# A two-layer sandwich kernel: the residual moved to VectorE, the flag count and the next block's norms moved in the order, the last store on another queue

## The chip, the cores and the metric

The kernel runs on one core of a Trainium2 chip. The metric is device time in microseconds for one execution; each run of a program gives one time, and a kernel's time is the median of its runs. A core has five engines that run side by side and meet through semaphores: TensorE (PE in the profile; its weight loads are PEld), VectorE (DVE), ScalarE (ACT), GpSimd (POOL) and SyncE (SP), which here only issues transfers. Each engine takes its instructions in the order in which the program lists them. PSUM is the small memory that TensorE writes its products to, in banks; SBUF is the working memory; DRAM is the chip's main memory.

## The reference

The input is x with 4 x 512 rows of 512 numbers, so 2048 rows. Two feed-forward layers follow each other, each between two layer norms, with a residual around it:

```
x = x + norm(attn(norm(x)))        # first layer
x = x + norm(ffn(norm(x)))         # second layer

attn(h): s = silu(h @ Wg.T)        # 1376 wide
         set the 688 entries of each row with the smallest |s| to 0
         return (s * (h @ Wu.T)) @ Wd.T
ffn(h):  return (silu(h @ Wg.T) * (h @ Wu.T)) @ Wd.T
```

norm subtracts a row's mean and divides by the root of its variance plus 1e-5. All numbers are 32-bit floats.

## The kernel before

**Tiles.** A tile is 128 rows of x; there are 16, numbered 0 to 15. Weights stay in SBUF in 128-row pieces. Most products are done by a scheme with seven half-size products in place of eight (class `Seven`, L133, for the gate and up products; `downs`, L234, for the down product). Such a scheme needs sums of the quarters of both operands. Those of the weights are worked out once and kept in DRAM (`presum`), those of the activations come from VectorE (`moving_sums`, L125, tiles named T; L634 to L636 in `Unit.down_sums`) or from GpSimd (`stationary_sums`, L117, tiles named D). The products are called p1 to p7.

**First layer.** It runs in eight units of two tiles (class `Unit`). A unit norms and transposes its tiles, does the gate product, the up product and a search for each row's threshold (`search`, L467), and later the down product (`finish`, L644), the output norm and the residual. The search is a short fixed number of steps. For rows where it doesn't settle, it writes a flag into the tile `flags`. Whether any flag is set is counted once: L885 sums the flags of each partition, L887 sums over the partitions with a 1-column matmul into a bank named pbad, and L889 writes the count as an integer into `badi`. At L916 every engine reads this integer into a register, and at L917 all branch: with a count of 0, as here, past a second, general version of the whole program. The result of the first layer goes to DRAM as x1.

**Second layer.** It runs in four blocks of four tiles (class `Block`, L657). `norm(k)` (L663) loads tile k of x1 (into xnb, three buffers, L368), takes its statistics (L104, L106: st_ib, mv_ib), adds the epsilon (L108), takes the power -0.5 on GpSimd (L110), scales (L115), transposes on TensorE into a bank ptb (L376, of two banks with the tag pt) and copies with ScalarE into xT (L378; two buffers, one for each half of the columns). `sums` (L673) builds T. Then come five calls of `pair` (L685), each of which does the gate and the up product for 256 of the 1376 columns and ends with the multiplication L705; after each, `down_sums` (L724, L119 to L122) builds D on GpSimd. `rest` (L707) does the last 96 columns in the banks pxrb and pyrb with adds into sgr (L154, L160, L161, L167, L168). In the source the norms of the next block stand between `rest` and `finish` (L740), which does the down product for two pairs of tiles: padb, pydb and pxdb are the three banks of a pair, written by L260 and L266, and yb the two output tiles. The banks of the tags pa, px and py exist twice each, so pxdb of the second pair takes the bank that pxrb has used.

**Output norm.** `out_norm` (L344) loads the residual tile (xr or xrb, two buffers), takes mean and power of the row, and has three endings. In the first layer (`dst is x1`) VectorE subtracts the mean (L359) and does multiply-by-rs and add-residual in one instruction (L360). In the second layer, VectorE does subtraction and multiplication (L115, within `layernorm`) and GpSimd adds the residual (L363). The very last tile (`pa` given) has its first half still in PSUM: VectorE subtracts the mean from the two halves (L353) and does multiply and add in one instruction (L356). All three store with SP's queue (L364). All other loads and stores go by SP's queue too. The order of tiles at the end of the last block is 14, 12, 15, 13.

**Order.** The program is recorded in source order and then put in order by a scheduler, which simulates a timeline with its own costs and moves instructions of an engine ahead where it thinks they are ready (`tc.block(schedule_with_timeline_sim=True)`). So the norms of a block are not bound to the place where the source has them. In the built order of the kernel before, the first two tiles of a block are transposed at the start of the block before it, where they then keep the two pt banks, and VectorE takes their statistics there; those of tiles 4, 5 and 6 stand as early as the end of the first layer. The count of flags stands where the first layer ends, with a wait of SP's queue for it at 441 us.

Of the kernel before, what the change touches and what calls it, by code (L numbers as in the profile page):

```python
# [9 lines left out]
F32 = mybir.dt.float32  # L10
BF16 = mybir.dt.bfloat16
I32 = mybir.dt.int32
AF = mybir.ActivationFunctionType
ALU = mybir.AluOpType
AX = mybir.AxisListType

P = 128
# [14 lines left out]
def sandwich_kernel(  # L32
# [17 lines left out]
    nc = tc.nc  # L50
# [5 lines left out]
    NTT = NT // P  # L56
    TB = 4
# [12 lines left out]
    const = ctx.enter_context(tc.tile_pool(name="const", bufs=1))  # L70
    small = ctx.enter_context(tc.tile_pool(name="small", bufs=5))
# [7 lines left out]
    onec = const.tile([P, 1], F32, name="onec")  # L79
# [10 lines left out]
    flags = const.tile([P, 2, NTT], F32, name="flags")  # L90
    x1 = dram.tile([NT, H], F32, name="x1")
# [3 lines left out]
    def bank(tag, nm):  # L95
        return psum.tile([P, 512], F32, tag=tag, name=nm)

    def moments(parts, nm, kind):

        n = len(parts)  # L100
        bufs = 1 if kind == "f" else 5
        st = small.tile([P, n, 6], F32, tag="st" + kind, name=f"st_{nm}", bufs=bufs)
        for i in reversed(range(n)):
            nc.vector.bn_stats(st[:, i, :], parts[i])  # L104
        mv = small.tile([P, 2], F32, tag="mv" + kind, name=f"mv_{nm}", bufs=bufs)
        nc.vector.bn_aggr(mv, st)  # L106
        ve = small.tile([P, 1], F32, tag="ve" + kind, name=f"ve_{nm}", bufs=bufs)
        nc.vector.tensor_scalar(ve, mv[:, 1:2], EPS, None, ALU.add)  # L108
        rs = small.tile([P, 1], F32, tag="rs" + kind, name=f"rs_{nm}", bufs=bufs)
        nc.gpsimd.tensor_tensor(rs, ve, nhalf, ALU.pow)  # L110
        return mv, rs

    def layernorm(dst, src, nm, kind):
        mv, rs = moments([src], nm, kind)
        nc.vector.tensor_scalar(dst, src, mv[:, 0:1], rs, ALU.subtract, ALU.mult)  # L115
# [9 lines left out]
    def moving_sums(eng, b11, b12, b21, b22, t1, t2, t3, t4):  # L125

        eng.tensor_sub(t1, b12, b11)
        eng.tensor_sub(t2, b22, t1)
        eng.tensor_sub(t3, b22, b12)
        eng.tensor_sub(t4, b21, t2)  # L130
        return dict(p1=b11, p2=b21, p3=b22, p4=t4, p5=t1, p6=t2, p7=t3)
# [102 lines left out]
    def downs(work, pairs, key, w_d, wr, res, dst, nm, final=False):  # L234
# [81 lines left out]
        def p4(part=slice(None)):  # L316
            product("p4", PX, None, part)
            for p in st[part]:
                tiles, left, last, pa, px, py, ya, yb = p
                rest(px, p, 1, lo)  # L320
                nc.vector.tensor_add(yb[:, lo], yb[:, lo], px)
                out_norm(work, tiles[1], yb, res, dst, nm)
# [21 lines left out]
    def out_norm(work, t, y, res, dst, nm, pa=None):  # L344


        xr = work.tile([P, H], F32, tag="xr", name=f"xr{nm}_{t}")
        nc.sync.dma_start(xr, res[ts(t, P), :])
        if pa is not None:
            parts = [pa, y[:, H2:]]  # L350
            mv, rs = moments(parts, f"o{nm}_{t}", "f")
            for i in range(2):
                nc.vector.tensor_scalar(  # L353
                    y[:, ts(i, H2)], parts[i], mv[:, 0:1], None, ALU.subtract
                )
            nc.vector.scalar_tensor_tensor(y, y, rs, xr, ALU.mult, ALU.add)  # L356
        elif dst is x1:
            mv, rs = moments([y], f"o{nm}_{t}", "o")
            nc.vector.tensor_scalar(y, y, mv[:, 0:1], None, ALU.subtract)  # L359
            nc.vector.scalar_tensor_tensor(y, y, rs, xr, ALU.mult, ALU.add)  # L360
        else:
            layernorm(y, y, f"o{nm}_{t}", "o")
            nc.gpsimd.tensor_add(y, y, xr)  # L363
        nc.sync.dma_start(dst[ts(t, P), :], y)  # L364

    def load_x(work, src, t, nm, tag="xn", bufs=3):
        xn = work.tile([P, H], F32, tag=tag, name=f"xn{nm}_{t}", bufs=bufs)
# [12 lines left out]
    class Unit:  # L380
# [258 lines left out]
        def pair(self):  # L639
            return (  # L640
                self.tiles, lambda k, c: self.dleft[k][:, c, :], lambda i: self.hT[i][1]
            )

    def finish(units, wr):  # L644

        u = units[0]
        steps = downs(u.work, [u.pair() for u in units], "a", a_wd, wr, x, x1, u.nm)

        def p2():
            steps[-3]()  # L650
            for u in units:
                a12, s2 = u.dleft["p3"], u.dleft["p6"]
                nc.vector.tensor_sub(a12, a12, s2)

        return steps[:-3] + [p2] + steps[-2:]

    class Block:  # L657
# [27 lines left out]
        def pair(self, a, lefts):  # L685

            nm = f"{self.nm}_{self.b}_{a}"
            pool, kw = (self.work, dict(tag="hT")) if a < 2 else (self.big, dict(tag="b5"))
            hT = pool.tile([P, 2, N], F32, name=f"hTb{nm}", **kw)
            self.h.append(hT)  # L690
            h = hT.rearrange("p f (q n) -> p (f q) n", q=2)
            sg = self.work.tile([P, 4, N2], F32, tag="w", name=f"sg{nm}", bufs=1)
            ms = []
            for k, left, c in zip("gu", lefts, (sg, h)):
                left = {p: w[:, :, ts(a, P)] for p, w in left.items()}
                m = Seven(f"{k}b{nm}", left, self.right, c[:, 1, :], c[:, 2, :], c[:, 3, :])
                m.first()
                ms.append(m)
            c11g, c11u = [m.second() for m in ms]
            nc.scalar.activation(sg[:, 0, :], c11g, AF.Silu)  # L700
            nc.vector.tensor_mul(h[:, 0, :], sg[:, 0, :], c11u)
            ms[0].third()
            nc.scalar.activation(sg[:, 1:, :], sg[:, 1:, :], AF.Silu)  # L703
            ms[1].third()
            nc.vector.tensor_mul(h[:, 1:, :], sg[:, 1:, :], h[:, 1:, :])  # L705

        def rest(self, left):  # L707

# [31 lines left out]
        def finish(self, which, wr, final=False):  # L740
# [11 lines left out]
            for f in downs(self.work, pairs, "f", f_wd, wr, x1, out, f"b{self.nm}", final):  # L752
                f()

    def layers(nm, general):
        with ExitStack() as sctx:
            wpool = sctx.enter_context(tc.tile_pool(name="w" + nm, bufs=1))
# [9 lines left out]
            def last_rows(w_d, layer):  # L767
                n = I - 2 * HF
                w = work.tile([P, H], F32, tag="wr", name=f"wr{layer}{nm}", bufs=1)
                nc.sync.dma_start(w[:n, :], w_d[2 * HF :, :])  # L770
                return w[:n, :]

            blocks = [Block(b, nm, big, work) for b in range(NTT // TB)]
# [18 lines left out]
            for q in range(2):  # L792
                b = [
                    wu[:, 2 * r : 2 * r + 2, k * Q : (k + 1) * Q] for r in range(2) for k in (q, 2 + q)
                ]
                t = [y[:, :, ts(q, Q)] for y in (t1, t2, t4)]
                right.append(moving_sums(nc.vector, *b, t[0], t[1], b[1], t[2]))
            badi = None
            if general:
                wr = last_rows(a_wd, 1)  # L800
                ones = big.tile([P, I], BF16, tag="b5", name="g_ones")
# [12 lines left out]
            else:  # L814
                wr = last_rows(a_wd, 1)
# [64 lines left out]
            if not general:  # L880
                for f in units[-1].turns():
                    f()

                bad = small.tile([P, 1], F32, tag="bad", name="bad", bufs=2)
                nc.vector.tensor_reduce(bad, flags, AX.XY, ALU.add)  # L885
                pb = bank("pt", "pbad")
                nc.tensor.matmul(pb[:1, :1], bad, onec, start=True, stop=True)  # L887
                badi = const.tile([1, 1], I32, name="badi")
                nc.vector.tensor_copy(badi, pb[:1, :1])  # L889
                units[-1].down_sums()  # L890
                for f in finish([units[-1]], wr):
                    f()
            wr = last_rows(f_wd, 2)
            t = work.tile([P, 3, 2, I - 2 * HF], F32, tag="S", name=f"wrs{nm}", bufs=1)
# [5 lines left out]
            for b, block in enumerate(blocks):  # L900
                last = b + 1 == len(blocks)
                for a in range(HC):
                    block.pair(a, lefts)
                    block.down_sums(a)
                block.rest(rest)
                if not last:
                    for k in range(TB):
                        blocks[b + 1].norm(k)
                    blocks[b + 1].sums()
                block.finish([0, 1], wr, last)  # L910

        return badi

    with tc.block(schedule_with_timeline_sim=True):
        badi = layers("", False)
        nbad = nc.values_load(badi[0:1, 0:1], min_val=0, max_val=2 * P * NTT)  # L916
        with tc.If(nbad > 0, label="general"):  # L917
            layers("g", True)

# [35 lines left out]
```

## Time and profile before

| what | value |
|---|---|
| median of 3 runs | 875.24 us (874.98 to 875.84) |
| the profiled execution's own time | 873.69 us |
| its span, first to last instruction | 871.9 us |
| granted TensorE clock | 0.997 of full speed |
| TensorE busy | 855.0 us, 98% of the span |
| VectorE, ScalarE, GpSimd busy | 526.8, 302.8, 117.7 us |
| SP's transfers | 112.21 MB, 38.4% of the DMA engines' time |

The profile is of one execution. A line of the timeline gives the start (us from the span's start), the duration, the engine, the line of the source, the operation, and what it wrote and read (names without buffer numbers), with the partitions and elements of both, and how many of a kind follow each other. Brackets give the time that the engine had stood idle before, and what it waited for. SPq is a transfer's issue on SP; the transfer itself lands later. L12 means line 12 of the kernel, and line numbers are those of the kernel before unless the text says otherwise. VectorE, ScalarE and GpSimd being idle costs nothing in itself. The matmuls overlap: one of 256 columns is shown with 0.38 us, but the next starts 0.216 us after it.

### The profile page before, as it was taken

Reading aid. Unit: us, or ns where it says so; the run is one execution under the profiler, and the core shown is the slowest. Engines: PE = TensorE matmul, PEld = TensorE weight load, DVE = VectorE, ACT = ScalarE, POOL = GpSimd, SP = SyncE. Lnnn points to the kernel's source line nnn. Section 1 sums busy time; section 2 is a strip of 40 time slices with the busy share of each in tenths; the row PEclk is TensorE's granted clock in tenths of the full one; section 3 lists DMA queues with packets and bytes.
Section 4 is the critical chain, followed back from the end, with each engine's and each line's share of the span. In section 5 each row is a group of like instructions: output and inputs, shape, how many; then the busy total and the mean of one; then the engine's idle time right before and its main releaser. Section 6 shows DMA issues by size and latency. Waiting matters only on the chain. (4 is left out here: it accounts for less than half of the span.)

```text
span 871.9 us, 10340 instructions
## 1 busy us (share of the span) xinstructions
PE 855.0 (98%) x3642; PEld 659.8 (76%) x3642; DVE 526.8 (60%) x1417; ACT 302.8 (35%) x601; POOL 117.7 (14%) x193
## 2 busy tenths in 40 slices
PE   9999999999999999999999999999999999999995
PEld 5655566767667676678877888888888888888884
DVE  5887787776939587667956444454346442444424
ACT  3465575647474756565111111011111112011100
POOL 1000000000000000000112211321203221132102
PEclk9999999999999999999999999999999999999998
DMA  9998513335133333388473004510055001430032
GB/s 335 366 330 335 180 54 122 121 102 166 59 121 111 113 121 103 121 299 286 142 251 130 0 1 144 172 42 0 1 175 170 2 1 48 137 124 1 1 120 78
DMA packets 60381, 112.97 MB, mean 130 GB/s; under 512 B 4704, under 2 KB 34528, under 8 KB 60320
## 3 DMA queue, kind: packets, MB, share of 16 engines
q1 hardware_dynamic: 60320, 112.21, 38.4%
q8 instruction: 31, 0.51, 0.2%
q14 instruction: 30, 0.25, 0.1%
HBM read 93.32 MB, written 18.87 MB: 129 GB/s over the span
## 5 line engine op out<-in xcount | busy, mean ns | idle before, releaser
L488 ACT ACTIVATE ja<-v,cur 128x1376 bf16<-128x1376 f32 x96 | 138.4, 1441 | 56.6 <-DVE cur L513 36.9
L436 PE MATMUL pg<-wg,xT 128*128 128x456 f32 (+1 forms) x384 | 154.8, 549 | 0.2 <-ACT p L440 0.2
L436 PEld LDWEIGHTS pg<-wg,xT 128*128 128x128 f32 x384 | 71.9, 190 | 62.7 <-issue 57.6
L144 PE MATMUL pxub<-T,wu 128*128 128x256 f32 x160 | 41.3, 380 | 2.0 <-DVE hTb L160 1.8
L144 PE MATMUL pau<-wu,xT 128*128 128x344 f32 x128 | 43.1, 453 | 0.0
L144 PE MATMUL pagb<-xTb,wg 128*128 128x256 f32 x160 | 41.4, 379 | 0.0
L144 PE MATMUL paub<-xTb,wu 128*128 128x256 f32 x160 | 41.3, 380 | 0.0
L144 PE MATMUL pxgb<-T,wg 128*128 128x256 f32 x160 | 41.2, 380 | 0.0
L260 PE MATMUL pad<-wd_p,hT 128*128 128x256 f32 x160 | 38.9, 380 | 0.9 <-DMA wd_p<-in_L_attn_w_down_dram 0.9
L440 ACT ACTIVATE p<-pg 128x456 f32<-128x456 f32 (+1 forms) x48 | 26.0, 544 | 38.3 <-PE pg L436 35.0
L260 PE MATMUL pydb<-wdb_p,D 128*128 128x256 f32 x160 | 37.8, 379 | 0.0
L119 POOL TENSOR_TENSOR D<-hTb 128x256 f32<-128x256 f32 x20 | 14.6, 729 | 169.7 <-DVE hTb L705 169.7
L110 POOL TENSOR_TENSOR rs_o<-ve_o,nhalf 128x1 f32<-128x1 f32 x16 | 11.6, 724 | 188.6 <-DVE ve_o L108 188.5
L260 PE MATMUL pxd<-wd_p,hT 128*128 128x256 f32 x160 | 36.8, 379 | 0.0
L260 PE MATMUL padb<-wdb_p,hTb 128*128 128x256 f32 x160 | 36.7, 379 | 0.0
L260 PE MATMUL pxdb<-wdb_p,hTb 128*128 128x256 f32 x160 | 36.2, 379 | 0.0
L260 PEld LDWEIGHTS pad<-wd_p,hT 128*128 128x128 f32 x160 | 29.9, 190 | 7.5 <-DMA wd_p<-in_L_attn_w_down_dram 1.3
L144 PEld LDWEIGHTS pxub<-T,wu 128*128 128x128 f32 x160 | 30.1, 190 | 6.9 <-DVE hTb L160 2.2
L260 PEld LDWEIGHTS pxd<-wd_p,hT 128*128 128x128 f32 x160 | 30.4, 190 | 5.5 <-issue 0.4
L703 ACT ACTIVATE sg<-sg 128x768 f32<-128x768 f32 x20 | 16.9, 843 | 49.0 <-DVE sg L168 49.0
L493 DVE TENSOR_SCALAR low<-cur 128x2 int32<-128x2 f32 x48 | 7.9, 165 | 42.6 <-ACT ja L488 42.2
L260 PEld LDWEIGHTS padb<-wdb_p,hTb 128*128 128x128 f32 x160 | 30.4, 190 | 4.3
(246 smaller groups left out, 1715.6 us busy)
## 6 DMA issues: line engine op xcount, KB each, us to landing
wd_p<-sum_a SPq DMA_DIRECT2D x28, 640.0 KB, 4.0
wd_p<-in_L_attn_w_down_dram SPq DMA_DIRECT2D x21, 640.0 KB, 4.0
wdb_p<-sum_f SPq DMA_DIRECT2D x16, 640.0 KB, 4.0
wdb_p<-in_L_ffn_W_down_dram SPq DMA_DIRECT2D x12, 640.0 KB, 4.1
xn<-in_x_dram SPq DMA_DIRECT2D x16, 256.0 KB, 4.1
xr<-in_x_dram SPq DMA_DIRECT2D x16, 256.0 KB, 3.9
x<-y SPq DMA_DIRECT2D x16, 256.0 KB, 3.2
xnb<-x SPq DMA_DIRECT2D x16, 256.0 KB, 4.1
```

The costliest lines, as they stand in the source:

```text
L110: nc.gpsimd.tensor_tensor(rs, ve, nhalf, ALU.pow)
L119: eng.tensor_add(s1, a21, a22)
L144: nc.tensor.matmul(ps, self.left[k][:, c, :], self.right[k][:, c, :], start=first and c == 0, stop=c == 1, skip_group_check=not first,)
L260: nc.tensor.matmul(p[which], p[1](k, c), ws[k][:, c, :], start=first and c == 0, stop=c == HC - 1, skip_group_check=not first,)
L436: nc.tensor.matmul(pg, self.xT[:, i, c, :], wg[:, c, c0:c1], start=(c == 0), stop=(c == NH - 1),)
L440: nc.scalar.activation(p[:, c0:c1], pg, AF.Silu)
L488: nc.scalar.activation(junk, v, AF.Sign, bias=cur[:, 0, i : i + 1], accum_out=cur[:, 1, i : i + 1],)
L493: nc.vector.tensor_scalar(low, cur[:, 1, :], 0.0, None, ALU.is_gt)
L703: nc.scalar.activation(sg[:, 1:, :], sg[:, 1:, :], AF.Silu)
```

## The change

Five things change. In `out_norm`, all second-layer tiles but the last now end as the first layer's do: VectorE subtracts the mean and then multiplies and adds the residual in one instruction, and GpSimd adds nothing; for the last tile nothing changes but its store, which goes by ScalarE's queue. The flag count is a function of its own, `count_bad`, and it is called after the first pair of the third block (number 2). The register read of the count (L916) is in it, so it no longer stands behind the whole layer code; VectorE's part of the read is kept in a list, and the last block's `finish` is issued behind it. `Block.pair` notes its last multiplication as `mark`, and the norms of the next block are issued behind the `mark` of the fifth pair. Issued behind means that the scheduler may not place those of the instructions that run on the named one's engine, VectorE here, ahead of it in that engine's order; no semaphore is added for it. The general version of the program has the same edits except for the flag count, and isn't executed here.

```diff
--- before.py
+++ after.py
@@ -353,15 +353,12 @@
                 nc.vector.tensor_scalar(
                     y[:, ts(i, H2)], parts[i], mv[:, 0:1], None, ALU.subtract
                 )
-            nc.vector.scalar_tensor_tensor(y, y, rs, xr, ALU.mult, ALU.add)
-        elif dst is x1:
+        else:
             mv, rs = moments([y], f"o{nm}_{t}", "o")
             nc.vector.tensor_scalar(y, y, mv[:, 0:1], None, ALU.subtract)
-            nc.vector.scalar_tensor_tensor(y, y, rs, xr, ALU.mult, ALU.add)
-        else:
-            layernorm(y, y, f"o{nm}_{t}", "o")
-            nc.gpsimd.tensor_add(y, y, xr)
-        nc.sync.dma_start(dst[ts(t, P), :], y)
+        nc.vector.scalar_tensor_tensor(y, y, rs, xr, ALU.mult, ALU.add)
+        queue = nc.sync if pa is None else nc.scalar
+        queue.dma_start(dst[ts(t, P), :], y)
 
     def load_x(work, src, t, nm, tag="xn", bufs=3):
         xn = work.tile([P, H], F32, tag=tag, name=f"xn{nm}_{t}", bufs=bufs)
@@ -702,7 +699,7 @@
             ms[0].third()
             nc.scalar.activation(sg[:, 1:, :], sg[:, 1:, :], AF.Silu)
             ms[1].third()
-            nc.vector.tensor_mul(h[:, 1:, :], sg[:, 1:, :], h[:, 1:, :])
+            self.mark = nc.vector.tensor_mul(h[:, 1:, :], sg[:, 1:, :], h[:, 1:, :]).ins
 
         def rest(self, left):
 
@@ -752,6 +749,19 @@
             for f in downs(self.work, pairs, "f", f_wd, wr, x1, out, f"b{self.nm}", final):
                 f()
 
+    def count_bad():
+
+        bad = small.tile([P, 1], F32, tag="bad", name="bad", bufs=2)
+        nc.vector.tensor_reduce(bad, flags, AX.XY, ALU.add)
+        pb = bank("pt", "pbad")
+        nc.tensor.matmul(pb[:1, :1], bad, onec, start=True, stop=True)
+        badi = const.tile([1, 1], I32, name="badi")
+        nc.vector.tensor_copy(badi, pb[:1, :1])
+        traced = nc.cur_bb.bb.instructions
+        k = len(traced)
+        nbad = nc.values_load(badi[0:1, 0:1], min_val=0, max_val=2 * P * NTT)
+        return nbad, [i for i in traced[k:] if i.engine == mybir.EngineType.DVE]
+
     def layers(nm, general):
         with ExitStack() as sctx:
             wpool = sctx.enter_context(tc.tile_pool(name="w" + nm, bufs=1))
@@ -795,7 +805,7 @@
                 ]
                 t = [y[:, :, ts(q, Q)] for y in (t1, t2, t4)]
                 right.append(moving_sums(nc.vector, *b, t[0], t[1], b[1], t[2]))
-            badi = None
+            nbad = None
             if general:
                 wr = last_rows(a_wd, 1)
                 ones = big.tile([P, I], BF16, tag="b5", name="g_ones")
@@ -880,13 +890,6 @@
             if not general:
                 for f in units[-1].turns():
                     f()
-
-                bad = small.tile([P, 1], F32, tag="bad", name="bad", bufs=2)
-                nc.vector.tensor_reduce(bad, flags, AX.XY, ALU.add)
-                pb = bank("pt", "pbad")
-                nc.tensor.matmul(pb[:1, :1], bad, onec, start=True, stop=True)
-                badi = const.tile([1, 1], I32, name="badi")
-                nc.vector.tensor_copy(badi, pb[:1, :1])
                 units[-1].down_sums()
                 for f in finish([units[-1]], wr):
                     f()
@@ -902,18 +905,24 @@
                 for a in range(HC):
                     block.pair(a, lefts)
                     block.down_sums(a)
+                    if b == 2 and a == 0 and not general:
+                        nbad, loads = count_bad()
                 block.rest(rest)
                 if not last:
-                    for k in range(TB):
-                        blocks[b + 1].norm(k)
+                    with tc.issue_after(block.mark):
+                        for k in range(TB):
+                            blocks[b + 1].norm(k)
                     blocks[b + 1].sums()
-                block.finish([0, 1], wr, last)
-
-        return badi
+                with ExitStack() as order:
+                    if last and not general:
+                        for i in loads:
+                            order.enter_context(tc.issue_after(i))
+                    block.finish([0, 1], wr, last)
+
+        return nbad
 
     with tc.block(schedule_with_timeline_sim=True):
-        badi = layers("", False)
-        nbad = nc.values_load(badi[0:1, 0:1], min_val=0, max_val=2 * P * NTT)
+        nbad = layers("", False)
         with tc.If(nbad > 0, label="general"):
             layers("g", True)
```

## The prediction

> **What bounds the kernel now.** The page's first part comes first: TensorE (PE) is busy for 855.0 of 871.9 us, so time can only be won where PE stands still or after it has finished.
>
> ```profile
> PE 855.0 (98%) x3642; PEld 659.8 (76%) x3642; DVE 526.8 (60%) x1417; ACT 302.8 (35%) x601; POOL 117.7 (14%) x193
> ```
>
> Where it stands still, and for whom, is in the waits of PE (time, count, longest). I leave out the start of the program, which the change doesn't touch.
>
> ```profile
> PE pxub L144 <- DVE hTb L160: 1.8, 1, 1.8
> PE ptb L376 <- DVE badi L889: 0.9, 1, 0.9
> PE pad L260 <- DMA wd_p<-in_L_attn_w_down_dram: 0.9, 1, 0.9
> PE pxub L144 <- DVE hTb L154: 0.2, 1, 0.2
> ```
>
> All four lie between 440 and 475 us, where the first layer hands over to the second. The timeline there shows the largest: VectorE (DVE) takes its instructions in order, and a statistic for a tile of a later block (st_ib) stands ahead of the L160 that PE needs.
>
> ```profile
> 465.17 0.40 SPq L368 DMA_DIRECT2D xnb<-x  x1
> 469.11 0.69 DVE L104 BATCH_NORM_STATS2 st_ib<-xnb 128x6 f32<-128x512 f32 x1 [4.24 <-DMA xnb<-x]
> 469.72 0.40 DVE L160 TENSOR_TENSOR hTb<-hTb,pxub 128x256 f32<-128x256 f32 x1
> 470.17 1.13 PE L144 MATMUL pxub<-T,wu 128*128 128x256 f32 x4 [1.83 <-DVE hTb L160]
> ```
>
> From start to start a 128x256 matmul takes 0.216 us. Subtracting that pitch, I get lost PE time of 1.08 us at 440.2 (and 0.31 at the next product, 0.12 beside pbad), 1.08 at 448.2, 1.99 at 470.2, 0.35 at 474.9, 0.19 at 669.6, and nothing of size in the four blocks besides.
>
> The end is a second stretch. PE's last matmul ends at 862.4, the span at 871.9. The timeline of the end:
>
> ```profile
> 859.41 0.42 SPq L348 DMA_DIRECT2D xrb<-x  x1
> 862.67 0.42 DVE L104 BATCH_NORM_STATS2 st_ob<-padb 128x6 f32<-128x256 f32 x1
> 863.44 0.47 DVE L353 TENSOR_SCALAR yb<-padb,mv_ob 128x256 f32<-128x256 f32 x1
> 863.83 1.43 DVE L353 TENSOR_SCALAR yb<-yb,mv_ob 128x256 f32<-128x256 f32 x1
> 863.85 1.26 POOL L363 TENSOR_TENSOR yb<-yb,xrb 128x512 f32<-128x512 f32 x1 [1.68 <-DMA xrb<-x]
> 865.07 0.60 POOL L110 TENSOR_TENSOR rs_ob<-ve_ob,nhalf 128x1 f32<-128x1 f32 x1
> 865.70 0.75 DVE L356 SCALAR_TENSOR_TENSOR yb<-yb,rs_ob,xrb 128x512 f32<-128x512 f32 x1 [0.44 <-POOL rs_ob L110]
> ```
>
> The last tile's power (L110) stands behind the residual add of the tile before it (L363), which waits for a load; and the add stretches DVE's second subtraction to 1.43 us.
>
> **What the Trainium skill says.** "SBUF — State Buffer", section "SBUF: two separate sides": VectorE and GpSimd share one port pair, held for a whole instruction, and the loser blocks. The trace agrees: 0.47 us without the add beside it, 1.43 with it. "DMA: Bandwidth & Descriptors", section "Anatomy of one DMA — SWDGE (gpsimd) path": about 2.0 us fixed, and bytes at 436 GB/s; for 256 KB I estimate 2.6 us from that. The trace's shortest load of a tile (xnb) takes 2.57 us, those beside other transfers up to 6.65. "Runtime: NRT & Kernel Launch", section "Instruction fetch mechanics": a taken branch can force a fetch of instructions. SyncE (SP) branches at L917 at 866.88, and its next record is at 870.00, though the last store had landed at 869.03.
>
> **The change part by part.** The built order of the changed program gives the positions; durations are those of the profile before.
>
> *Norms behind the fifth pair.* Statistics, powers and scalings of the next block leave the earlier stretches.
> (a) 440 us: tiles 4, 5, 6 leave DVE's queue here, each 0.69 + 0.18 + 0.15 + 0.55 = 1.57 us. The new order first joins PE's at the add L329 of y_10, whose last matmul now ends at 429.85. From there to L634, the sum that PE needs, stand 20 instructions, 8.3 us by their spacing in the trace, so L634 ends at about 438.9. PE arrives at 438.9. Saved: 1.08 + 0.31 + 0.12 - 0.07 = 1.43 us (bounds 0.4 to 1.5); the badi instructions leave the same place.
> (b) 448 us: the weights load is issued when PE frees its buffer, and PE wants it 3.68 us later. It took 4.73 behind an x tile's load issued at 441.0. That load goes; undisturbed ones of this size took 3.80 to 4.26. At 4.0 the wait falls from 1.08 to 0.35: 0.7 saved (0 to 1.1).
> (c) 470 and 475 us: no st_ib ahead of L160. pxub's product ends at 467.3, L160 by 467.9, and PE does another product until 468.2: 1.99 + 0.35 = 2.33 saved (2 to 2.3).
> (d) 669.6: 0.19 saved. Transposes of 0.87 us per block move from its start to the end of the block before: the same PE work, no gain.
>
> What is late next: at the end of blocks 0 to 2 the two moved transposes now stand just ahead of the second pair's p1 product. Call their start t0 (before, padb starts there, 732.27 in block 2). The fourth tile's load reuses the first tile's buffer, so SP issues it at t0 + 0.63 (a load at 402.18 followed its transpose of 401.55). DVE's order is now L161, st_ib of that fourth tile, its L106 and L108, then L167; and PE's pxdb of the second pair needs L167, which frees its PSUM bank. PE reaches it after two transposes (0.87), padb (2.16), pxrb and pyrb (0.86 each): t0 + 4.75. How long DVE and PE take once the tile lands, block 2's start shows in the same pattern:
>
> ```profile
> 668.09 0.69 DVE L104 BATCH_NORM_STATS2 st_ib<-xnb 128x6 f32<-128x512 f32 x1 [3.58 <-DMA xnb<-x]
> 669.11 0.41 DVE L160 TENSOR_TENSOR sg<-sg,pxgb 128x256 f32<-128x256 f32 x1
> 669.57 1.13 PE L144 MATMUL pxgb<-T,wg 128*128 128x256 f32 x4
> ```
>
> That is 1.48 us. So PE stalls for 0.63 + L + 1.48 - 4.75 = L - 2.64 us, three times, with L the landing. SP's queue is idle at that point, and the next weights load comes 2.6 us later, so I take a nearly undisturbed 2.9: 0.26 a block, 0.8 lost. The bounds are L = 2.57 (no loss) and 5.4 (8.3 us).
> The first three tiles stand behind the fifth pair's sums on GpSimd (POOL), which end at 729.15; the power and L115 add about 1.3, and the transpose comes at 732.27: 1.5 us of cover.
>
> *Residual on DVE.* Fifteen tiles trade L115 (0.55) and POOL's L363 (1.27) for a subtraction (0.5) and a multiply-add (0.75). DVE gets 0.7 us more a tile at a 60% load. New is that DVE itself waits for xrb. At a block's start the second tile's multiply-add comes ahead of L154 hTb: store at 761.5, load at 761.9, landing by 766.0 to 767.0 (4.1 to 5.1 us there), so L154 ends at 767.1 to 768.1; PE needs it at 769.85. Cost nothing, with 1.7 us of cover.
> In the end stretch: tile 14's multiply-add ends at 857.85, its store and the next xrb are issued 1.13 us earlier than before, landing (4.28) at 862.55. PE ends at 862.42; st_ob 862.46, tile 15's multiply-add 862.84, L106 863.50, L108 863.72, subtractions to 864.55, the power beside them 863.96 to 864.52. The last xrb (issued 860.71, 3.05 to 4.28) is there by 863.8 to 865.0. The last multiply-add starts at 864.58 instead of 865.70: 1.1 saved (0.7 to 1.1).
>
> *Last store on ScalarE's queue.* "DMA: Bandwidth & Descriptors", section "Issuing engines are not separate DMA queues", promises only sequencer time; no run here shows a ScalarE store. SP (0.34 an issue) may branch some 2.9 us sooner, but ScalarE, which branched at 857.80 under cover, now stores, reads the count (0.46) and branches after 865.4. Such a branch took 2.4 to 3.6 us to the next record. Between -0.8 (sooner) and +0.8; I take 0.2 saved.
>
> *Flag count in block 2.* Its two tiny matmuls move at no cost. The read on SP (0.49) lies in front of loads not needed for 90 us. DVE's read moves ahead of L282 in block 3, 0.5 us where L161 has 2 us to spare. Free.
>
> Sum: 1.43 + 0.7 + 2.33 + 0.19 + 1.1 + 0.2 - 0.8 = 5.15 us, against a profiled execution of 873.69 (span 871.9), whose successor I put at 868.5. The median shown, 875.24, lies 1.55 above that execution; the same saving from it gives 870.1.
>
> **Rivals.**
> A, the forecast: 870.1.
> B, the handover's stalls only shift: PE finds the next late operand at 440 and 448 (nothing from a and b), the rest as in the sum: 872.2. For it: DVE is busiest there. Against: 4.7 us of its work leave.
> C, block ends: L is 4.1, the median of all xnb loads, so 1.46 a block, 4.4 in all: 873.7; at 4.6, 875.2. For it: median and traffic elsewhere. Against: those loads shared the queue.
> D, slower: the same wait, with L at 5.4 as at 636.8 us: 8.3 lost, 877.6. The point where the gain is gone is L = 4.6.
> E, the end gives nothing because ScalarE's branch is then the last: 871.4.
> "Doesn't do what it says" is out: the built order has the moves.
>
> **How the numbers follow.** A change within 0.2% (1.75 us, about what a measurement here can tell from none) is the same. A 0.5, B 0.15, E 0.17, C 0.13 (half of it just below 873.5, half above), D 0.05. Faster: 0.5 + 0.15 + 0.17 + 0.06 = 0.88, lowered to 0.84 for waits I haven't found; same 0.1; slower 0.06. The range runs from the good ends of b, block ends and end stretch (868.0) to C (873.7).
>
> **What would show it.** No PE waits at 440 and 470; st_ib only behind L705; a PE wait for L167 three times at 0.3 us; no L363; the last multiply-add 2.2 us behind PE's last matmul. Wrong would make it: PE waits of over 1.5 us for L167, xrb ahead of L154 by more than 1.7, or ScalarE last at the end.

## The result and the profile after

The changed kernel takes 867.47 us (median of 6 runs, 866.6 to 868.34), the kernel before beside it 875.54 (6 runs, 872.08 to 876.46). The ratio is 0.9913, with a 95% interval from 0.9895 to 0.9931: 0.9% faster, so the forecast's sign was right, but the time lies half a microsecond below its range. The profiled execution of the changed kernel takes 867.17 us, its span is 865.4 us, 6.5 below the 871.9 of before. Line numbers of the changed kernel are 3 below those of before from L363 to L751; the multiply-add of every tile is now L359, the subtraction of all but the last L358, the store L361.

From the page of the changed kernel, the busy times:

```profile
PE 854.2 (99%) x3642; PEld 659.6 (76%) x3642; DVE 533.7 (62%) x1432; ACT 302.5 (35%) x601; POOL 98.8 (11%) x178
```

VectorE has 15 instructions more and GpSimd 15 fewer, as the sum said. TensorE's waits after the program's start (total, count, longest):

```profile
PE pyd L260 <- DVE D L631: 0.3, 1, 0.3
PE ph L607 <- ACT xTb L375: 0.3, 1, 0.3
PE ph L607 <- ACT hT L612: 0.3, 1, 0.3
PE pg L433 <- ACT p L437: 0.2, 1, 0.2
```

None of the four waits of before is among them; these four lie ahead of the handover, the first three at 398.8, 431.3 and 396.7 us. At the handover, the timeline shows L631 (L634 of before) ending just ahead of the product that needs it, and two short stops that are left, 0.31 us ahead of 437.54 and 0.23 ahead of 445.21:

```profile
437.54 1.13 PE L144 MATMUL paub<-xTb,wu 128*128 128x256 f32 x4
...
437.83 0.83 DVE L631 TENSOR_TENSOR D<-hT 128x640 f32<-128x640 f32 x1 [0.25 <-ACT hT L612]
...
438.94 2.32 PE L260 MATMUL pyd<-wd_p,D 128*128 128x256 f32 x10
...
441.29 0.38 SPq L231 DMA_DIRECT2D wd_p<-in_L_attn_w_down_dram  x1
...
445.21 2.43 PE L260 MATMUL pad<-wd_p,hT 128*128 128x256 f32 x10
```

L631 ends at 438.66. The weights that the product at 445.21 needs were issued at 441.29, 3.9 us ahead of it. The block ends have the wait that the forecast looked for. In the first block:

```profile
522.79 0.80 SPq L365 DMA_DIRECT2D xnb<-x  x2
...
525.66 0.70 DVE L104 BATCH_NORM_STATS2 st_ib<-xnb 128x6 f32<-128x512 f32 x1 [2.43 <-DMA xnb<-x]
...
526.68 0.41 DVE L167 TENSOR_TENSOR sgr<-sgr,pxrb 96x256 f32<-96x256 f32 x1
...
527.14 2.02 PEld L260 LDWEIGHTS pxdb<-wdb_p,D 128*128 128x128 f32 x10 [0.48 <-DVE sgr L167]
527.14 2.43 PE L260 MATMUL pxdb<-wdb_p,D 128*128 128x256 f32 x10
```

The fourth tile's statistic waits for its load, L167 stands behind it, and the product comes 0.22 us late. And the end, where the last multiply-add now starts 2.3 us behind TensorE's last matmul (857.90), and ScalarE issues the store:

```profile
859.53 0.61 POOL L110 TENSOR_TENSOR rs_ob<-ve_ob,nhalf 128x1 f32<-128x1 f32 x1 [1.17 <-DVE ve_ob L108]
859.76 0.34 DVE L353 TENSOR_SCALAR yb<-yb,mv_ob 128x256 f32<-128x256 f32 x1
860.20 0.75 DVE L359 SCALAR_TENSOR_TENSOR yb<-yb,rs_ob,xrb 128x512 f32<-128x512 f32 x1
860.98 0.38 ACTq L361 DMA_DIRECT2D out_dram<-yb  x1
```

### The profile page after: what moved, and what is told of

Its sections match the earlier page's. It is cut to its first block, busy times and chain, and to the rows that moved or that the text cites. A ratio compares the mean times of both kernels' runs of the same rounds, so it can differ in the third digit from the quotient of the medians.

```text
span 865.4 us, 10342 instructions
## 1 busy us (share of the span) xinstructions
PE 854.2 (99%) x3642; PEld 659.6 (76%) x3642; DVE 533.7 (62%) x1432; ACT 302.5 (35%) x601; POOL 98.8 (11%) x178
## 4 chain that ended last, share of the span: by engine, by line
PE 51%; DVE 2%; ACT 1%; DMA 1%; issue 0%; POOL 0%; ACTq 0%; DVEq 0%
PE pxub L144 6%; PE pxgb L144 6%; PE pxdb L260 6%; PE paub L144 4%; PE pagb L144 4%; PE pydb L260 4%; PE pyub L144 4%; PE pygb L144 4%; PE padb L260 3%; PE pxd L260 2%; PE pyd L260 2%; PE pxrb L144 1%; PE pad L260 1%; ACT ja L485 1%; PE parb L144 1%; PE ptb L373 1%
## 5 line engine op out<-in xcount | busy, mean ns | idle before, releaser
L144 PEld LDWEIGHTS paub<-xTb,wu 128*128 128x128 f32 x160 | 30.3, 190 | 4.5 <-ACT sg L697 0.4
L260 PEld LDWEIGHTS pxdb<-wdb_p,hTb 128*128 128x128 f32 x160 | 30.4, 190 | 4.2
```

What stands on the lines that cost most here:

```text
L144: nc.tensor.matmul(ps, self.left[k][:, c, :], self.right[k][:, c, :], start=first and c == 0, stop=c == 1, skip_group_check=not first,)
L260: nc.tensor.matmul(p[which], p[1](k, c), ws[k][:, c, :], start=first and c == 0, stop=c == HC - 1, skip_group_check=not first,)
```

## The experiments

Two readings stand against each other. F is the forecast's sum. T is what the two traces say: TensorE's stretch and the end won more than F has. In the expectations below, T's numbers are those of the traces known by then.

To compare traces I cut each at four points. The fixed point is the start of the seven transposes (ph) at 431.42 us of before: TensorE does the same 1640 matmuls ahead of it in all the kernels (their order differs only among the last 22, and in held_further from 70 us on), and it stops there for 0.46 us in every trace. The others are the end of TensorE's last matmul, the start of the last multiply-add, and the end of the span. The ratio is that of the times, each against the kernel before on the same chip.

| kernel | up to the fixed point | to PE's last matmul | to the last multiply-add | to the end | ratio, interval |
|---|---|---|---|---|---|
| before | 431.42 | 431.00 | 3.28 | 6.19 | |
| before_again | 430.94 | 432.12 | 3.44 | 6.16 | 0.9997 (0.9978 to 1.0016) |
| norms_only | 433.21 | 426.42 | 3.13 | 6.16 | 0.9929 (0.9907 to 0.9951) |
| residual_only | 431.91 | 429.60 | 2.29 | 6.03 | 0.9979 (0.9969 to 0.9989) |
| store_only | 431.12 | 431.17 | 3.42 | 5.43 | 1.0009 (0.9995 to 1.0023) |
| after | 431.26 | 426.64 | 2.30 | 5.19 | 0.9913 (0.9895 to 0.9931) |
| after_again | 434.03 | 426.67 | 2.30 | 5.41 | 0.9941 (0.9924 to 0.9958) |
| count_at_old_place | 431.84 | 426.64 | 2.29 | 5.38 | 0.9933 (0.9910 to 0.9955) |
| after_store_on_sync | 431.86 | 426.66 | 2.30 | 5.94 | 0.9944 (0.9929 to 0.9959) |
| block1_norms_free | 432.36 | 429.55 | 2.30 | 5.32 | 0.9956 (0.9942 to 0.9969) |
| scalar_reads_early | 430.34 | 426.45 | 2.30 | 4.99 | 0.9921 (0.9908 to 0.9934) |
| tile4_behind | 433.09 | 426.02 | 2.29 | 5.25 | 0.9904 (0.9881 to 0.9928) |
| two_orders | 432.99 | 426.03 | 2.30 | 5.06 | 0.9930 (0.9913 to 0.9947) |
| held_further | 433.62 | 426.77 | 2.30 | 5.69 | 0.9936 (0.9916 to 0.9956) |

The first column moves by 3.7 us between traces, the others by little once the norms are held. The table is therefore the better witness for differences below 2 us, and the times for the whole. What differs between executions of the same work is called a draw below.

**Norms alone (norms_only).** The kernel before with:

```diff
-            nc.vector.tensor_mul(h[:, 1:, :], sg[:, 1:, :], h[:, 1:, :])
+            self.mark = nc.vector.tensor_mul(h[:, 1:, :], sg[:, 1:, :], h[:, 1:, :]).ins
...
-                    for k in range(TB):
-                        blocks[b + 1].norm(k)
+                    with tc.issue_after(block.mark):
+                        for k in range(TB):
+                            blocks[b + 1].norm(k)
```

> The kernel before with one part of the change: the next block's norms queued behind the fifth pair. Traces so far (T): the four stalls of TensorE between 440 and 475 us and the one at 669 are gone, except what the flag count still costs at 440 (0.1 to 0.5 us), and the block ends cost 0.3 us in all; TensorE's last matmul ends 3.9 to 4.4 us earlier, the end stretch behind it stays 9.5 us: about 0.4 to 0.5% below before. The forecast's sum (F) has 3.85 less the flag count's share. Rival B (the stalls at the handover only shift): 2.0 us, 0.2%. Rival C (block ends cost 4.4 us in all): no gain.

Measured: the time fell by 0.71%, TensorE's stretch by 4.58 us, and the end stretch is 9.29 us (before: 9.47). That is a little above T and well above rival B, and rival C is out. The size carries the draw of the waits at 440 and 448 us: set against the other traces with the old order of the norms (before_again, store_only, residual_only), it is 3.2 to 5.7. The norms are the bulk of the change.

**Residual alone (residual_only).** The kernel before with the three endings of `out_norm` made one, as in the change, and the store left on SP.

> The kernel before with one part of the change: subtraction and multiply-add on VectorE in every output norm, last store still on SyncE's queue. F and T: TensorE's stretch keeps its length within 0.5 us; the last multiply-add starts 2.2 to 2.3 us behind TensorE's last matmul instead of 3.28, so 1.0 us saved, about 0.1%. Rival: VectorE's waits for the residual tiles reach TensorE at the block starts, and TensorE's last matmul ends later by 1 us or more.

Measured: the last multiply-add starts 2.29 us behind TensorE's last matmul, as both expected: 1.0 us saved. TensorE's stretch came out 1.4 us shorter, which neither expected. Of this, 1.1 us lies in the waits at 440 and 448 us. That part is a draw: up to 554 us all engines of this kernel run the same instructions in the same order as before's, so the edit can't have made it. The other 0.3 is the wait at 669 us, which is gone here; there the edit has changed VectorE's order, and L160 stands ahead of L106 and L108. No wait of TensorE came with VectorE's waits for the residual tiles, so that rival is out.

**Store alone (store_only), and the store back on SP (after_store_on_sync).**

```diff
-        nc.sync.dma_start(dst[ts(t, P), :], y)
+        queue = nc.sync if pa is None else nc.scalar
+        queue.dma_start(dst[ts(t, P), :], y)
```

> The kernel before with one part of the change: the last store on ScalarE's queue. F: 0.2 us saved (between -0.8 and +0.8). T: SyncE's row of semaphore steps after its branch (1.1 us in the trace of before, behind its late branch) now runs while ScalarE still fetches behind its own branch, so from the start of the last multiply-add to the span's end 5.2 us instead of 6.2: 1.0 saved, about 0.1%. The share is read from the trace's end, since 0.1% is near what the times can tell.

> The kernel after with the last store back on SyncE's queue. T: SyncE branches after the store, some 3 us of fetch, then its own row of semaphore steps (1.1 us): from the start of the last multiply-add to the span's end 6.0 us instead of 5.2, so 0.8 us slower than after. F (the forecast): 0.2 us slower.

Measured: the times can't tell these kernels from their partners (1.0009 beside 1; 0.9944 beside 0.9941). The last column can: 0.76 us less with the store on ScalarE (6.19 to 5.43), and 0.5 to 0.75 more with it back on SP (5.94 against 5.41 and 5.19). T had the size right within 0.3; F's 0.2 was too small. The instructions of the branch line, and of the line behind the branches (L951, in the kernel after L960), show why. First the kernel before (count, then shortest, median and longest duration in ns, and the first and last start):

```profile
L917 SPq EVENT_SEMAPHORE  x8: 17/17/17, 870.0 to 870.5; - x8
...
L917 SPq COMPARE_BRANCH  x1: 45/45/45, 866.9 to 866.9; - x1
...
L951 SPq EVENT_SEMAPHORE  x10: 17/28/28, 870.6 to 871.8; - x10
```

Then the kernel after:

```profile
L926 SPq EVENT_SEMAPHORE  x8: 17/17/17, 862.5 to 863.4; - x8
...
L926 SPq COMPARE_BRANCH  x1: 45/45/45, 859.6 to 859.6; - x1
...
L926 ACTq COMPARE_BRANCH  x1: 54/54/54, 861.9 to 861.9; - x1
...
L926 ACTq EVENT_SEMAPHORE  x1: 17/17/17, 864.5 to 864.5; - x1
...
L960 SPq EVENT_SEMAPHORE  x10: 17/28/655, 863.5 to 865.3; - x10
```

SP has a row of sixteen semaphore steps behind its branch (the eight of L917 and eight of L951), 1.1 us from 870.0 on in the kernel before, with only the common stop of all engines behind it. In the kernel after, SP branches at 859.6, goes through most of that row by 863.9 and waits 0.65 us for ScalarE, which is back at 864.5. So the late branch moved to an engine with no such row. The store back on SP confirms it: there SP is back 4.04 us behind the start of the last multiply-add, sooner than ScalarE in the kernel after (4.30), and still the end comes later, because the row stands behind it. The Trainium skill, "Runtime: NRT & Kernel Launch", section "Instruction fetch mechanics", says that a taken branch can have to wait until its target is fetched; the pause behind it is 2.6 us on ScalarE and 2.9 on SP in this trace, which fits. That the pause is a fetch is not shown: GpSimd's next record comes 0.46 us after its branch in the same trace.

**Flag count at its old place (count_at_old_place).** The kernel after with `count_bad` called where the turns of the eighth and last unit end, as before (the expectation calls it the fourth), and with the registers read at the very end.

> The kernel after with one part undone: the flag count traced with the fourth unit and read at the very end, as before. F: free to move, except its share at 440 us: the count's copy stands ahead of the sum that TensorE needs, 0.1 to 0.5 us lost there. T: the same, and VectorE's and SyncE's reads of the count (0.5 to 0.8 us) come back at the end without reaching the last store, so 0.1 to 0.6 us in all above the kernel after; rival: the reads at the end lie on the path and cost 1 us more.

Measured: TensorE's stretch is the same to 0.03 us, and the end lies within what two traces of after span. But the equality is a coincidence: this trace loses 0.41 us at 842.7 us, in a stop that the traces of after don't have. By the places of the count, the old one was the better by 0.2 to 0.4 us (norms_only, which has it there too, takes 426.42). In block 2 its two small matmuls cost 0.2. At the old place they cost 0.2 as well, but they fill a stop there: without them TensorE waits for ScalarE's L697, which costs 0.41 in the kernel after. So the move wasn't quite free, and the cost that F saw at the old place, a wait behind the count's copy, doesn't show once the norms are held.

**After once more, and before once more (after_again, before_again).**

> The kernel after once more, beside many runs of the kernel before. Traces so far (T): the true distance is the 6.3 to 6.5 us of the spans (ratio 0.9926), the 8.07 of the first comparison came partly from the draw of the kernel before (875.5 there, 873.9 beside the parts of the change). Rival: 8 us (ratio 0.991) stands, and the profiled execution of before was a lucky one by 1.6 us.

> The kernel before, unchanged, for a second trace. T: from the fixed point at 431 us to TensorE's last matmul 430 to 431.5 us again, with 2.3 us lost at 470 to 475 and a varying loss at 440 and 448; the time up to the fixed point is anything from 430 to 434. Rival: the waits at 440 and 448 are the same as in the first trace to 0.1 us.

Measured: 868.83 us for after (6 runs, 866.3 to 871.45), 874.14 for before beside it, ratio 0.9941. Both intervals hold 0.9925 to 0.993, which is where T put it; the rival's 0.991 lies outside the second. From the fixed point to the end, after takes 434.13 and 434.38 us, before 440.47 and 441.71: 6.1 to 7.6 us apart, 6.8 on average, 0.78%. The two traces of after differ by 3.0 us, and 2.8 of it lies ahead of the fixed point, in work that the change leaves alone. The timeline of after_again shows the largest pieces of it:

```profile
71.60 1.49 DVE L217 TENSOR_TENSOR ps_g_w<-ps_g_w,ps_g_z 128x1280 f32<-128x1280 f32 x1 [3.72 <-DMA ps_g_w<-in_L_ffn_W_gate_dram]
...
73.01 0.51 DVE L154 TENSOR_TENSOR c<-c,pxu 128x344 f32<-128x344 f32 x1
...
73.57 1.42 PE L144 MATMUL pxu<-wu,xT 128*128 128x344 f32 x4 [1.98 <-DVE c L154]
74.83 2.41 PE L144 MATMUL pau<-wu,xT 128*128 128x344 f32 x4
```

A sum of weights that waits for its load stands ahead of an add that TensorE needs: 2.15 us lost here, 0.07 in the first trace of after, 1.05 in the first of before. Then the next four matmuls take 2.41 us instead of the 1.3 to 1.4 of four such matmuls elsewhere: from 74.92 to 78.33 us the granted clock of TensorE is half of full speed in this trace (0.54 on average over 75.0 to 78.6), which costs another 1.7 us; why it fell isn't shown. No other trace has a half clock between the first stretch of full clock and TensorE's last matmul, so this trace is an unusually long one. And of the waits at the handover, those at 440 and 448 us vary too. In before_again:

```profile
PE ptb L376 <- DVE badi L889: 1.3, 1, 1.3
PE pad L260 <- DMA wd_p<-in_L_attn_w_down_dram: 1.3, 1, 1.3
```

Both were 0.9 in the first trace of before, and in store_only, where the order up to there is the same, they are 1.6 and 0.3. So the rival to before_again falls: a trace shows a draw of these two waits. They make 432.12 us from the fixed point to TensorE's last matmul, above T's 430 to 431.5.

**Only the second block's norms free (block1_norms_free).**

```diff
-                    with tc.issue_after(block.mark):
+                    with tc.issue_after(block.mark) if b else ExitStack():
```

> The kernel after, but the norms of the second block (traced in the first) aren't held behind the fifth pair; those of blocks 2 and 3 are. T: the waits of TensorE at 440 (0.7 to 1.5), 448 (0.3 to 0.9 more) and 470 to 475 us (2.3) return, so 3.3 to 4.7 us slower than after; the held norms of the other two blocks are worth at most 0.2. Rival: the gain comes from VectorE's relief in all the blocks, and a third or less of it (1.5 us) is lost here.

Measured: TensorE's stretch is 2.9 us longer than after's. The ratio is 0.9956 beside 0.9941, which their intervals can't tell apart. The size is under T's range, since the waits at 470 and 475 us didn't return. In the waits of TensorE:

```profile
PE pyd L260 <- DVE ve_ib L108: 1.7, 1, 1.7
PE pad L260 <- DMA wd_p<-in_L_attn_w_down_dram: 1.3, 1, 1.3
```

The statistic that stood ahead of L160 at 469 us was tile 8's, the first of the third block, and that one is still held. So T's attribution was wrong, and the run splits the gain by block: 2.9 us hang on the second block's norms, and the waits at 470 and 475 us on the third's. The rival that the gain comes evenly from VectorE's relief in all blocks (1.5 at most here) is out.

**The wait at the block ends taken away (tile4_behind).** The norm of the fourth tile is issued behind L167 (`block.last`) instead of behind the fifth pair:

```diff
                     with tc.issue_after(block.mark):
-                        for k in range(TB):
+                        for k in range(3):
                             blocks[b + 1].norm(k)
+                    with tc.issue_after(block.last):
+                        blocks[b + 1].norm(3)
```

> The kernel after, with the norm of each block's fourth tile queued on VectorE behind the add (L167) that frees the bank for TensorE's next product, instead of in front of it: this takes the wait at the block ends away. F (the forecast's landing of 2.9 us): TensorE wins 0.26 us at each of three block ends, 0.8 in all. T: the landings in the traces of after are 2.6 to 2.85 us and the waits 0.0 to 0.22, so 0.2 to 0.35 us in all from the fixed point at 431 us to TensorE's last matmul (426.4 us instead of 426.65). Rival: the tile's transposes now come late, and as much is lost again.

Measured: 426.02 us, 0.62 and 0.65 less than the two traces of after. The timeline of the first block end:

```profile
528.03 0.42 DVE L167 TENSOR_TENSOR sgr<-sgr,pxrb 96x256 f32<-96x256 f32 x1 [3.03 <-PE pxrb L144]
528.37 0.68 DVE L104 BATCH_NORM_STATS2 st_ib<-xnb 128x6 f32<-128x512 f32 x1
528.69 2.32 PE L260 MATMUL pxdb<-wdb_p,D 128*128 128x256 f32 x10
```

L167 is now early and the product waits for nothing, so the rival is out. The block ends had cost about 0.6, nearer to F's 0.8 than to T's 0.2 to 0.35. T had counted the waits alone; each comes with 0.10 us more, as the second matmul behind a wait starts 0.320 us after the first instead of 0.216. One sees it in the groups: ten matmuls take 2.43 us after a wait and 2.32 without.

**Two ways to go further (scalar_reads_early, two_orders), and one that fails (held_further).** The first issues ScalarE's read of the count early as well, so that it no longer stands between the last store and ScalarE's branch:

```diff
-        return nbad, [i for i in traced[k:] if i.engine == mybir.EngineType.DVE]
+        return nbad, [i for i in traced[k:] if i.engine in (mybir.EngineType.DVE, mybir.EngineType.Activation)]
```

> The kernel after with ScalarE's read of the flag count (0.48 us, between the last store and the branch) in front of the last two pairs' products too, as VectorE's already is. T: ScalarE branches 0.5 us sooner and is back by the time that the store has landed and SyncE's steps are done: 0.4 to 0.5 us faster than after, 4.7 to 4.8 us from the last multiply-add's start to the end. Rival: the landing of the store (2.3 to 3.1 us behind its issue) is what ends last, and nothing is gained.

> The kernel after with the two orders that helped alone: ScalarE's read of the flag count early, and the norm of the fourth tile behind the add at the block end. T: from the fixed point at 431 us to TensorE's last matmul 426.0 us (after: 426.65), and 7.2 to 7.3 us from there to the end (after: 7.5 to 7.7), so 0.8 to 1.0 us below after; beside the kernel before 7.0 to 7.2 us less, ratio 0.992. Rival: the two don't add, and 433.9 or more remains from the fixed point to the end.

Measured: 4.99 us from the last multiply-add to the end, 0.2 to 0.4 below after, a little under T: ScalarE branches 0.5 us sooner but came back 2.9 us later instead of 2.6 to 2.8. With the fourth tile's norm held as well (two_orders), fixed point to end is 433.39, 0.7 to 1.0 below after, as T had it for the sum of both; its rival (433.9) is out. By the times (0.9921 and 0.9930) neither can be told from after; that they are better stands on the trace alone.

The last one adds to these two that the weight sum L217 of the second layer's gate weights (key g), the one that stood ahead of TensorE's add at 72 us, is issued behind a multiplication of the unit's second half:

```diff
+        with ExitStack() as order:
+            if key == "g":
+                order.enter_context(tc.issue_after(mark))
+            nc.vector.tensor_sub(w, w, z)
-        nc.vector.tensor_sub(w, w, z)
```

> The kernel after with three more orders: ScalarE's read of the count early, the fourth tile's norm behind the add at the block end, and in the first unit but one the last of the summed gate weights (1.49 us of VectorE behind a load of 4 to 8 us) queued behind the product of that unit's second half. T: the wait of TensorE at 71 to 74 us, 0.0 to 2.15 us in ten traces with a mean of 0.9, is gone, the block ends win 0.2 to 0.3 and the end 0.4: 1.5 us below after on average (ratio to before 0.990 to 0.992) and a narrower spread of times. Rival: VectorE's later 1.49 us delays the next products' adds, and the wait only moves to 77 to 80 us.

Measured: TensorE doesn't wait at 72 us any more, and loses 1.56 us at 126 to 131 (0.3 in most others), 0.96 at 399 and 0.86 at 414 us; up to the fixed point it takes 433.62, within the 430.3 to 434.0 of the others. Its end is longer too (5.69): ScalarE is back 3.1 us behind its branch and VectorE 3.9, later than in any other kernel here. Of its waits:

```profile
PE ph L610 <- ACT he L617: 0.8, 1, 0.8
PE pxd L263 <- DVE y L285: 0.7, 1, 0.7
PE pyd L263 <- DVE D L634: 0.4, 1, 0.4
```

Its ratio is 0.9936, so no gain shows. The rival had the place wrong (77 to 80), but waits elsewhere are what its idea asks for. How much of them is due to the edit and how much to the draw of loads, one trace can't say: a loss at 397 to 400 us stands in several others.

## Why the prediction was right or wrong

**Right.** What bounds the kernel, the four waits and their removal, the position of each moved norm, the wait for L167 at three block ends, VectorE's waits for xrb staying hidden, GpSimd's add off the path, a last multiply-add that starts 2.3 us (forecast 2.2) behind TensorE: all are in the trace of after. Rivals B, C and D are out (norms_only, tile4_behind), though 0.41 us of B came true, a new wait at 437.5. E is half true: ScalarE is indeed the last to branch, which the prediction had named as a sign of being wrong, but the end gains all the same. The gain of the end stretch rests on the add L363 being gone. The pair of figures given for it, 0.47 and 1.43 us, is of two instructions, one on a half in PSUM and one on a half in SBUF; the second takes 0.34 in the trace of after. And the add doesn't stretch every instruction of VectorE: the statistic L104 beside the add of 860.22 took 0.69 us, as ever.

**The sum was 1.35 short of the traces (5.15 against 6.5).** By its terms, first traces, each wait with its 0.10 us:

| term | forecast | measured |
|---|---|---|
| (a) 440 us | 1.43 | 1.74 of before less 0.41 of a new wait at 437.5 for ScalarE's L697: 1.33 |
| (b) 448 us | 0.7 | 1.18 less 0.33: 0.85 |
| (c) 470 and 475 us | 2.33 | 2.54 |
| (d) 669.6 us | 0.19 | 0.29 |
| block ends | -0.8 | -0.57 by the gaps, about -0.6 by tile4_behind |
| flag count | 0 | -0.20 at its new place; what it cost at the old one is within (a) |
| residual, end stretch | 1.1 | 0.98 |
| last store on ScalarE | 0.2 | 0.5 to 0.8 |

TensorE's stretch gained 4.36, against 3.85 in the sum; the terms measured add to 4.24, and the rest is in small pieces. The last column of the first table gained 1.0. The store explains 0.5 to 0.8 of that. The other 0.2 to 0.5 may be the reads of the count that no longer stand there, or a draw: two traces of after differ by 0.22 here. Another 0.16 of the 6.5 lies ahead of the fixed point.

**The step that failed by size** is "Last store on ScalarE's queue": "ScalarE, which branched at 857.80 under cover, now stores, reads the count (0.46) and branches after 865.4". It set the new late branch against the old one and took them as equals. It left out what came behind SP's branch in the trace of before, the row of semaphore steps, and took 0.2 where 0.5 to 0.8 were measured. The bounds (up to 0.8) held it; the value taken, close to their middle, had no mechanism behind it. Second come the block ends, 0.2 cheaper than forecast, with 2.7 to 2.9 us from the load's issue to the statistic (the 2.6 that the prediction estimates for such a load comes from a section on transfers that GpSimd issues; here SP issues them, and the three landings are 2.63 to 2.85), and the 0.10 us that a removed wait carries and that the sum left out (0.2 in (c), 0.1 in (d)). "Its two tiny matmuls move at no cost" was wrong by 0.2 the other way: they cost that in block 2.

**The step that failed the range** is "The median shown, 875.24, lies 1.55 above that execution; the same saving from it gives 870.1". The 875.24 was a median of three, and such medians are draws: beside the parts of the change the kernel before had 873.88 (35 runs), then 874.14, 874.04 and 873.35, and after had 867.47 and then 868.83. (The sets ran on several chips, each beside its own runs of before; how much of the spread is the chips' isn't separated.) The range was put together from the bounds of the terms and left out this spread, more than 1 us to either side. Those bounds, 0.4 us better for (b), 0.8 for the block ends and 0.6 for the store, put its low end at 868.3, not at 868.0; from a base of 874 it would lie at 867.1, below the time measured. The sum of 5.15 gives 868.9 from that base, beside the 868.0 that the twelve runs of after have as their median. So of the 2.6 us that the result lies below the forecast, about 1 us is the sum and the rest the draw of the two medians. Some small slips in the working change nothing: (a) adds to 1.44 and (c) to 2.34, and the cover of the moved tiles at 732.27 is 1.8 us, not 1.5.

## What to carry to other kernels

Where a scheduler puts an instruction that waits for a load ahead of one that the bounding engine needs, binding it behind a late instruction on the same engine can take the wait away, as it did here at 470 us; check what stands behind it at the new place (here 0.6 us at the block ends), and whether a further bind (here behind L167) takes that away too. At a program's end, look not only at who branches last but at what that engine still has to do behind its branch. Keep the spread of medians of few runs apart from the bounds of the mechanism, and put both into the range.

## What the runs showed of the hardware that was not expected

A stop of TensorE ahead of 128x256 matmuls costs 0.104 us beyond the wait: the first gap between them behind it is 0.320 us instead of 0.216, at every wait behind the fixed point in before, after and tile4_behind, even where the stop itself was 0.04 us or less (629 and 732 us of after). Behind the stop ahead of the 128x128 transposes at 431 us it is 0.056 us, 0.165 instead of 0.109. In two other traces a loss below 0.1 us comes without it (527.9 of count_at_old_place, 734.7 of after_again). After a taken branch at the end, the next record on the same engine came 2.4 to 2.8 us later on ScalarE (2.9 to 3.1 in the three kernels that read the count early there), 2.9 to 3.1 on SP and 2.9 to 3.9 on VectorE, but after 0.46 us on GpSimd in the kernel after. And work that nothing in the change touches took 430.3 to 434.0 us between executions. In the longest, 2.15 us are a wait behind a load and 1.7 us a stretch of 3.4 us for which the granted clock was half of full speed.
